# A GRU feeding a mixture of experts: gates in three stages with a bank each, one bank for transposes, and another order of the shared units' pieces

## The chip, the core and the metric

The kernel runs on one core of one Trainium2 chip. Its five engines work side by side, each through its own queue in order: TensorE (PE in the profile, with its weight loads as PEld) multiplies, VectorE (DVE) and ScalarE (ACT) do elementwise work, GpSimd (POOL) copies and issues indirect DMAs, and SyncE (SP) issues DMAs. The metric is the time of one execution on the device in microseconds; the median of three executions stands for the kernel.

## The reference

The input x has 8 sequences of 256 tokens of 512 floats. A GRU runs over the 256 steps, all 8 sequences at once; its states go through a feed-forward layer, and the result is added to x.

```python
def cell(h, x):
    gi = x @ W_ih + b_ih
    gh = h @ W_hh + b_hh
    i_r, i_z, i_n = jnp.split(gi, 3, axis=-1)
    h_r, h_z, h_n = jnp.split(gh, 3, axis=-1)
    r = jax.nn.sigmoid(i_r + h_r)
    z = jax.nn.sigmoid(i_z + h_z)
    n = jnp.tanh(i_n + r * h_n)
    h_new = (1.0 - z) * n + z * h
    return (h_new, h_new)
...
    # 8 experts of width 256, the best 2 for each token, weights renormalised
    routed = jnp.einsum('te,eth->th', combine, eo)
    shared = _silu_and_mul(x @ w_sh_gate_up) @ w_sh_down    # width 1024
    return (routed + shared).reshape(orig_shape)
```

All of it is in float32. The state of a step is needed in full before the gates of the next, so the 256 steps are a chain.

## The kernel before, in words

The 256 steps are cut into 16 blocks (k) of 16 steps: 16 steps of 8 sequences are 128 rows. The input projections (`x @ W_ih`) of a block are made while the block before runs and go out to DRAM; they come back as "seeds", four steps (a chunk) at a time, through SP's queue, a chunk ahead of their use (`load_seeds`, `turn_seeds`, lines 320 to 333). The shared part of the feed-forward layer for block k-1 is computed during block k; the routed part only after the last step, as 39 tiles of 128 rows (`tile_unit`), each with the weights of one expert. Both work on float32.

A step (`step`, lines 348 to 388) does this. TensorE multiplies the transposed state hT by the recurrent weights, in column groups of 32 that run side by side, each with a weight load of 8 columns: 16 matmuls for gates r and z together into `ps_rz` (128x256), then 16 for n into `ps_n` (128x128). In the trace each matmul is two records, so a gate group has 32. The accumulators were filled before with the input part, by copies on ScalarE (`open_gates`, lines 337 to 343), as soon as the step before had read them. Then VectorE transposes r,z (L364), ScalarE takes the sigmoid (L366), VectorE transposes n (L370), multiplies by r (L372), adds the input part (L373), ScalarE takes tanh (L375), and VectorE computes 1 - z (L379), z * h (L381), (1 - z) * n (L382) and the sum, the new state (L383). GpSimd copies it into the block's rows, `hc` (L386).

Between one step's matmuls and the next, TensorE works on pieces from a queue. The order is written out by hand at build time, not found by a scheduler: each piece has an assumed cost (0.86 for a full matmul piece, MM, and 0.12 for a transpose, TR), and in each step as many pieces are taken, whole or in halves, as spread the queue evenly over the remaining steps (lines 777 to 798). A block's queue has first the next block's projections (12 matmul pieces and the transposes of x, L245), then four shared units. A unit (`unit`, lines 570 to 605) has up to four stages: transposes of its input (only for routed tiles), four up pieces (L260, `gu_s`) with the gating on ScalarE and VectorE behind them (L566 to L568), two transposes of the activation with a copy by ScalarE (L589, L591), and two down pieces (`po`, again at L260). The fourth unit's down pieces end with an addition on VectorE (L618) and the store of the block's output by SP (L619). Some steps have routing work too: the router's matmuls (`choose`, L398), the places of tokens (L451, L453), and the transposes of the block's states (`send_rows`, L491).

`feed` (lines 709 to 719) interleaves the stages of successive units. Given a new unit, it queues the new one's first stage, then two up pieces of the unit fed before it, the transposes of the one before that, the other two up pieces, and that one's down pieces. Its calls per block are the four shared units and None, so a block's fourth unit has its transposes and down pieces as the first shared pieces of the next block, one right behind the other. Transposes take their accumulators from the pool `ps_t`, which has two buffers.

After the last step the fourth unit of block 14 and the shared units of block 15 run together with the last routing work (lines 801 to 821), and then the routed tiles.

Of the kernel before, what the change touches and what calls it, by code (L numbers as in the profile page):

```python
# [9 lines left out]
F32 = mybir.dt.float32  # L10
# [3 lines left out]
ALU = mybir.AluOpType  # L14
# [3 lines left out]
P = 128  # L18
# [7 lines left out]
def kernel(  # L26
# [42 lines left out]

    nc = tc.nc
    B, T, D = x.shape
    G3 = w_ih.shape[1]
# [20 lines left out]
    dram = ctx.enter_context(tc.tile_pool(name="dram", bufs=1, space=bass.MemoryType.DRAM))  # L95
    ps_gru = ctx.enter_context(tc.tile_pool(name="ps_gru", bufs=1, space=PSUM))
    ps_mm = ctx.enter_context(tc.tile_pool(name="ps_mm", bufs=3, space=PSUM))
    ps_t = ctx.enter_context(tc.tile_pool(name="ps_t", bufs=2, space=PSUM))
    ps_o = ctx.enter_context(tc.tile_pool(name="ps_o", bufs=1, space=PSUM))
    ctx.enter_context(tc.manual_schedule())  # L100

# [128 lines left out]

    ps_rz = ps_gru.tile([P, 2 * P], F32, name="ps_rz")
    ps_n = ps_gru.tile([P, P], F32, name="ps_n")
    for ps in (ps_rz, ps_n):
        n = ps.shape[-1]
        nc.tensor.matmul(ps, seeds[0][:, 0, 0:P], seeds[0][:, 0, 0:n], start=True, stop=True)


    xT_of = {}  # L240

    def transpose_x(k):
        ps = ps_t.tile([P, NQ, P], F32, tag="tp", name=f"xTp_{k}")
        for q in range(NQ):
            nc.tensor.transpose(ps[:, q, :], x_tiles[k][:, q * P : (q + 1) * P], ident)  # L245
        xT = two.tile([P, NQ, P], F32, tag="xrT", name=f"xT_{k}")
        nc.scalar.copy(xT, ps)  # L247
        xT_of[k] = xT
        x_tiles.pop(k)
        if k + 2 < NB:  # L250
            load_x(k + 2)

    by_groups = [True]

    def multiply(ps, lhs, rhs, start, stop):

# [77 lines left out]

    nT_of = {}

    def open_gates(n, part):

        c, t = divmod(n, SC)
        if part == 0:  # L340
            nc.scalar.copy(ps_rz, seeds[c % NS][:, t, 0 : 2 * P])  # L341
        else:
            nc.scalar.copy(ps_n, seed_hn)  # L343

    whh_v = whh.rearrange("p q (a j i) -> p q a j i", j=4, i=32)
    hc_of = {}
# [1 line left out]
    def step(n):  # L348
        k, t = divmod(n, TS)
        c, ts = divmod(n, SC)  # L350
        hT, new = states[n % NH], states[(n + 1) % NH][:, :, 0:B]
        for ps, lo, hi in ((ps_rz, 0, 2 * NQ), (ps_n, 2 * NQ, 3 * NQ)):
            for q in range(NQ):
                for j in range(4):
                    nc.tensor.matmul(  # L355
                        ps[32 * j : 32 * j + B, :].rearrange("p (a i) -> p a i", i=32),
                        hT[:, q, 0:B],
                        whh_v[:, q, lo:hi, j, :],
                        start=False,
                        stop=(q == NQ - 1),  # L360
                        skip_group_check=True,
                    )
        gT = state.tile([P, 2 * NQ, 32], F32, tag="gT", name=f"gT_{n}")
        nc.vector.transpose(gT.rearrange("p a b -> p (a b)"), ps_rz)  # L364
        rz = state.tile([P, 2 * NQ, B], F32, tag="rz", name=f"rz_{n}")
        nc.scalar.activation(rz, gT[:, :, 0:B], AF.Sigmoid)  # L366
        if n + 1 < T:
            open_gates(n + 1, 0)
        gn = state.tile([P, NQ, 32], F32, tag="gn", name=f"gn_{n}")
        nc.vector.transpose(gn.rearrange("p a b -> p (a b)"), ps_n)  # L370
        nt = state.tile([P, NQ, B], F32, tag="nt", name=f"nt_{n}")
        nc.vector.tensor_tensor(nt, gn[:, :, 0:B], rz[:, 0:NQ, :], ALU.mult)  # L372
        nc.vector.tensor_tensor(nt, nT_of[c][:, ts, :, 0:B], nt, ALU.add)  # L373
        nn = state.tile([P, NQ, B], F32, tag="nn", name=f"nn_{n}")
        nc.scalar.activation(nn, nt, AF.Tanh)  # L375
        if n + 1 < T:
            open_gates(n + 1, 1)
        omz = state.tile([P, NQ, B], F32, tag="omz", name=f"omz_{n}")
        nc.vector.tensor_scalar(omz, rz[:, NQ:, :], -1.0, 1.0, ALU.mult, ALU.add)  # L379
        zh = state.tile([P, NQ, B], F32, tag="zh", name=f"zh_{n}")  # L380
        nc.vector.tensor_tensor(zh, rz[:, NQ:, :], hT[:, :, 0:B], ALU.mult)  # L381
        nc.vector.tensor_tensor(nn, omz, nn, ALU.mult)  # L382
        nc.vector.tensor_tensor(new, nn, zh, ALU.add)  # L383
        if t == 0:
            hc_of[k] = two.tile([P, NQ, P], F32, tag="hc", name=f"hc_{k}")
        nc.gpsimd.tensor_copy(  # L386
            hc_of[k].rearrange("p q (b t) -> p q b t", t=TS)[:, :, :, t], new
        )
# [97 lines left out]
    def send_rows(k):  # L486

        hc = hc_of[k]
        ps = ps_t.tile([P, D], F32, tag="tp", name=f"hrp_{k}")
        for q in range(NQ):  # L490
            nc.tensor.transpose(ps[:, q * P : (q + 1) * P], hc[:, q, :], ident)  # L491
        hr = two.tile([P, D], F32, tag="y", name=f"hr_{k}")
        nc.scalar.copy(hr, ps)
        nc.sync.dma_start(rows[:, k * TS : (k + 1) * TS, :], hr)
# [6 lines left out]
    def lay_tiles(part_no):  # L501
# [43 lines left out]
        elif part_no == 1:  # L545
            ps = ps_mm.tile([P, NT], F32, tag="mm", name="exp")
            nc.tensor.matmul(ps, ones, laid["spread"], start=True, stop=True)
            steer = small([NT], "steer", I32)
            nc.vector.tensor_scalar(steer, ps, float(E - 1), None, ALU.min)
            laid["steer"] = steer  # L550
        else:
            ps = ps_t.tile([P, 2, P], F32, tag="tp", name="listp")
            for v in range(2):
                nc.tensor.transpose(ps[:, v, :], laid["got"][:, :, v], ident)
            row = small([NT], "row", I32)
            nc.vector.tensor_copy(row, ps[:, 0, 0:NT])
            share = small([NT], "share")
            nc.vector.tensor_copy(share, ps[:, 1, 0:NT])
            laid.update(row=row, share=share)
# [10 lines left out]
    def unit(name, box, lhs, w_up, w_down_, done, before_=None, multiply=nc.tensor.matmul):  # L570
        def up(q, cols):
            if q == 0 and cols.start == 0:
                box["ps"] = ps_mm.tile([P, 2 * IM], F32, tag="mm", name=f"gu_{name}")
            multiply(  # L574
                box["ps"][:, cols],
                lhs(q),
                w_up(q)[:, cols],
                start=(q == 0 and cols.start == 0),
                stop=(q == NQ - 1 and cols.stop == D),
            )  # L580

        def up_end():
            box["act"] = three.tile([P, IM], F32, tag="act", name=f"act_{name}")
            gated(box["ps"], box["act"])

        def turn():
            ps = ps_t.tile([P, NF, P], F32, tag="tp", name=f"actTp_{name}")
            for f in range(NF):
                nc.tensor.transpose(ps[:, f, :], box["act"][:, f * P : (f + 1) * P], ident)  # L589
            actT = two.tile([P, NF, P], F32, tag="actT", name=f"actT_{name}")  # L590
            nc.scalar.copy(actT, ps)  # L591
            box["actT"] = actT

        def down(f, cols):
            done(f, cols, box["actT"][:, f, :], w_down_(f)[:, cols])

        return (
            [(NQ * TR, before_)] if before_ else [],
            [
                matmul_piece(lambda cols, q=q: up(q, cols), up_end if q == NQ - 1 else None)  # L600
                for q in range(NQ)
            ],
            [(NF * TR, turn)],
            [matmul_piece(lambda cols, f=f: down(f, cols)) for f in range(NF)],
        )
# [47 lines left out]
    def tile_unit(i):  # L653
        box = {}

        def before_():
            ps = ps_t.tile([P, NQ, P], F32, tag="tp", name=f"xrTp_{i}")
            xr = xr_of.pop(i)
            for q in range(NQ):
                nc.tensor.transpose(ps[:, q, :], xr[:, q * P : (q + 1) * P], ident)  # L660
            xrT = two.tile([P, NQ, P], F32, tag="xrT", name=f"xrT_{i}")
            nc.scalar.copy(xrT, ps)  # L662
            box["xrT"] = xrT
            fetch_rows(i + 2)
# [44 lines left out]
    def feed(stages):  # L709
# [1 line left out]

        last, oldest = under_way["up"], under_way["turn"]
        ups = last[1] if last else []
        queue.extend(stages[0] if stages else [])
        queue.extend(ups[: NQ // 2])
        queue.extend(oldest[2] if oldest else [])
        queue.extend(ups[NQ // 2 :])
        queue.extend(oldest[3] if oldest else [])
        under_way.update(up=stages, turn=last)

    def fill():
        while queue:
# [8 lines left out]
    for c in range(NS):  # L731
        load_seeds(c)
        if c == 0:
            turn_seeds(0)
    for part_no in range(2):
        open_gates(0, part_no)
    load_shared()

    projections = deque()
# [7 lines left out]
    for k in range(NB):  # L747
# [24 lines left out]
            queue.append(projections.popleft())  # L772
        assert k == NB - 1 or len(projections) <= 13 * (NB - 2 - k), "the next block's are made"
        if k > 0:
            for u in [*(shared_unit(k - 1, c, NSH) for c in range(NSH)), None]:
                feed(u)
        over = 0.0
        for t in range(TS):
            n = k * TS + t
# [17 lines left out]
            over = -room if t < TS - 1 else 0.0  # L797
        fill()
    by_groups[0] = False

    k = NB - 1
    load_again(k)
# [7 lines left out]
        (20 * MM, lambda k: lay_tiles(2)),  # L810
        (20 * MM, lambda k: fetch_rows(0)), (20 * MM, lambda k: fetch_rows(1)),
    ]
    for u in [*(shared_unit(k, c, NSH) for c in range(NSH)), None, None]:
        feed(u)
    spent = 0.0
    while queue or routing:
        while routing and (spent >= routing[0][0] or not queue):
# [38 lines left out]
```

## Time and profile before

| | us |
|---|---|
| three executions, median (lowest to highest) | 1552.07 (1550.34 to 1553.20) |
| profiled execution | 1548.32 |
| its span, first to last instruction | 1546.5 |
| TensorE busy in the span | 1487.6 (96%) |
| VectorE, ScalarE, GpSimd busy | 688.4, 359.6, 210.5 |
| from the first gate matmul of the first step to the router's matmuls after the last | 35.7 to 1276.3 |
| first matmul of the first routed tile | 1309.5 |
| mean granted TensorE clock | 0.992 |

A row of the page's costliest groups names the line, engine and operation, what is written and read with its shape, the count, then busy time and the mean length in ns of one, and after the second bar the idle time of the engine just before, with what ended it. A row of the timeline has the start, the length, the engine, the operation, how many instructions were merged into the row, and in brackets the idle time before it with what ended it. Matmuls overlap and their ends are modelled, so the step from one start to the next is the time that TensorE spent. A row of busy times by stretch has the stretch, its length, busy time and count of TensorE, its weight loads, VectorE, ScalarE and GpSimd, then the granted clock, the share of DMA and GB/s.

### The profile page before, as it was taken

What the parts mean: (1) busy time and instruction counts of PE and PEld (TensorE: products, weight loads), DVE (VectorE), ACT (ScalarE), POOL (GpSimd) and SP (SyncE); (2) the same over time, 40 slices, a digit from 0 to 9 for tenths busy, and PEclk for the clock granted to TensorE, in tenths of its full rate; (3) what the DMA queues carried; (4) which work ended last, traced back from release to release, by engine and by line L of the source; (5) the groups of instructions that cost most, each with busy time, mean ns of one, the idle gap of its engine ahead of it and who ended that gap; (6) DMA issues with size and microseconds to landing.
All of it is one profiled execution on the core that took longest, in us unless ns stands there. A gap on an engine that the chain in (4) does not pass through costs nothing.

```text
span 1546.5 us, 53864 instructions
## 1 busy us (share of the span) xinstructions
PE 1487.6 (96%) x22969; PEld 778.0 (50%) x22969; DVE 688.4 (45%) x2747; ACT 359.6 (23%) x1351; POOL 210.5 (14%) x419
## 2 busy tenths in 40 slices
PE   4999999999999999999999999999999999999997
PEld 1455555555555555555555555555555544444443
DVE  2445454545454445454545454545454542222222
ACT  0222222222222222222222222222222221222221
POOL 2001110101000001010101010101010102444443
PEclk8999999999999999999999999999999999999998
DMA  7613130303020202010201010101010314445454
GB/s 256 201 40 108 14 87 13 100 13 101 13 60 13 60 13 59 14 52 15 57 16 50 17 41 18 48 18 48 18 53 13 84 49 135 75 89 96 84 93 62
DMA packets 59055, 92.70 MB, mean 60 GB/s; under 512 B 8960, under 2 KB 29504, under 8 KB 58816
## 3 DMA queue, kind: packets, MB, share of 16 engines
q1 hardware_dynamic: 48056, 66.89, 14.8%
q0 software_dynamic: 10624, 22.10, 7.7%
q8 instruction: 182, 2.98, 0.8%
q14 instruction: 57, 0.47, 0.1%
q10 hardware_dynamic: 136, 0.26, 0.1%
HBM read 57.85 MB, written 31.37 MB: 58 GB/s over the span
## 4 chain that ended last, share of the span: by engine, by line
PE 91%; DVE 4%; issue 2%; ACT 1%; DMA 1%; DVEq 0%; SPq 0%; POOLq 0%; POOL 0%; ACTq 0%
PE ps_rz L355 29%; PE ps_n L355 15%; PE gu_s L260 12%; PE gip L260 10%; PE gu_t L574 9%; PE po L260 6%; PE yp L679 4%; PE actTp_s L589 1%; DVE gn L370 1%; PE xrTp L660 1%; PE lgp L398 1%; ACT nn L375 1%; DMA x<-in_x_dram 1%; DVE nt L372 1%; DVE nt L373 1%
## 5 line engine op out<-in xcount | busy, mean ns | idle before, releaser
L355 PE MATMUL ps_rz<-we,hT 128*8 128x256 f32 x8192 | 491.2, 380 | 21.4 <-DVE hT L383 10.8
L355 PEld LDWEIGHTS ps_rz<-we,hT 128*8 128x8 f32 x8192 | 223.2, 89 | 298.8 <-ACT ps_n L343 56.3
L364 DVE STREAM_TRANSPOSE gT<-ps_rz 128x256 f32<-128x256 f32 x256 | 115.2, 450 | 397.2 <-PE ps_rz L355 397.1
L355 PE MATMUL ps_n<-we,hT 128*8 128x128 f32 x8192 | 271.9, 273 | 0.0
L260 PE MATMUL gu_s<-wsu,hc 128*32 128x512 f32 (+2 forms) x2376 | 257.0, 518 | 0.0
L355 PEld LDWEIGHTS ps_n<-we,hT 128*8 128x8 f32 x8192 | 225.9, 90 | 53.2 <-issue 0.5
L366 ACT ACTIVATE rz<-gT 128x64 f32<-128x64 f32 x256 | 65.6, 256 | 710.1 <-DVE gT L364 710.1
L386 POOL COPY hc<-hT 128x32 f32<-128x32 f32 x256 | 62.3, 243 | 1111.4 <-DVE hT L383 1111.4
L260 PE MATMUL gip<-we,xT 128*32 128x512 f32 (+1 forms) x1952 | 189.7, 510 | 2.1 <-ACT xT L247 2.1
L574 PE MATMUL gu_t<-we,xrT 128*128 x312 | 146.7, 593 | 0.2 <-ACT xrT L662 0.2
L260 PE MATMUL po<-wsd,actT_s 128*32 128x512 f32 (+2 forms) x1132 | 131.2, 532 | 13.3 <-ACT actT_s L591 13.3
L370 DVE STREAM_TRANSPOSE gn<-ps_n 128x128 f32<-128x128 f32 x256 | 81.1, 317 | 122.5 <-PE ps_n L355 115.2
L260 PEld LDWEIGHTS gu_s<-wsu,hc 128*32 128x32 f32 (+1 forms) x2376 | 77.2, 111 | 89.2 <-issue 79.4
L375 ACT ACTIVATE nn<-nt 128x32 f32<-128x32 f32 x256 | 58.7, 229 | 185.1 <-DVE nt L373 185.1
L341 ACT COPY ps_rz<-seeds 128x256 f32<-128x256 f32 x256 | 94.5, 369 | 22.0 <-DMA seeds<-gid_rz 21.5
L260 PEld LDWEIGHTS gip<-we,xT 128*32 128x32 f32 x1952 | 58.0, 110 | 72.2 <-issue 60.9
L567 DVE TENSOR_TENSOR act_t<-gu_t,act_t 128x256 f32<-128x256 f32 x39 | 16.6, 424 | 146.3 <-ACT act_t L566 146.3
L685 POOL DMA_INDIRECT out_dram<-y,row x39 | 61.6, 1579 | 124.7 <-DVE y L682 95.8
L679 PE MATMUL yp<-we,actT_t 128*128 x156 | 73.4, 593 | 0.5 <-ACT actT_t L591 0.5
L574 PEld LDWEIGHTS gu_t<-we,xrT 128*128 128x128 f32 x312 | 53.3, 190 | 38.7 <-issue 38.0
L260 PEld LDWEIGHTS po<-wsd,actT_s 128*32 128x32 f32 (+1 forms) x1132 | 38.0, 112 | 57.8 <-issue 33.5
L343 ACT COPY ps_n<-seed_hn 128x128 f32<-128x128 f32 x256 | 66.4, 259 | 0.0
(139 smaller groups left out, 974.1 us busy)
## 6 DMA issues: line engine op xcount, KB each, us to landing
gid_rz<-gi SPq DMA_DIRECT2D x16, 512.0 KB
seeds<-gid_rz SPq DMA_DIRECT2D x256, 32.0 KB
we<-in_L_ffn_w_gate_up_dram SPq DMA_DIRECT2D x8, 1024.0 KB
gid_n<-gi SPq DMA_DIRECT2D x16, 256.0 KB
seeds_n<-gid_n SPq DMA_DIRECT2D x256, 16.0 KB
wsu<-_L_ffn_w_sh_gate_up_dram SPq DMA_DIRECT2D x8, 512.0 KB
rows<-hr SPq DMA_DIRECT2D x16, 256.0 KB
again<-in_x_dram SPq DMA_DIRECT2D x16, 256.0 KB
```

Source lines behind the costliest of these rows:

```text
L260: nc.tensor.matmul(ps[rows_], lhs[:, rows_], rhs, start=start, stop=stop, skip_group_check=True)
L341: nc.scalar.copy(ps_rz, seeds[c % NS][:, t, 0 : 2 * P])
L343: nc.scalar.copy(ps_n, seed_hn)
L355: nc.tensor.matmul(ps[32 * j : 32 * j + B, :].rearrange("p (a i) -> p a i", i=32), hT[:, q, 0:B], whh_v[:, q, lo:hi, j, :], start=False, s ...
L364: nc.vector.transpose(gT.rearrange("p a b -> p (a b)"), ps_rz)
L366: nc.scalar.activation(rz, gT[:, :, 0:B], AF.Sigmoid)
L370: nc.vector.transpose(gn.rearrange("p a b -> p (a b)"), ps_n)
L375: nc.scalar.activation(nn, nt, AF.Tanh)
L386: nc.gpsimd.tensor_copy(hc_of[k].rearrange("p q (b t) -> p q b t", t=TS)[:, :, :, t], new)
L574: multiply(box["ps"][:, cols], lhs(q), w_up(q)[:, cols], start=(q == 0 and cols.start == 0), stop=(q == NQ - 1 and cols.stop == D),)
L679: nc.tensor.matmul(box["y"], lhs, rhs, start=(f == 0), stop=(f == NF - 1))
L685: nc.gpsimd.indirect_dma_start(out=out.rearrange("b t d -> (b t) d"), out_offset=bass.IndirectOffsetOnAxis(ap=laid["row"][:, i : i + 1], a ...
```

## The change

The gates are worked on in three stages, r, n, z, each with an accumulator of its own bank: r and z become matmuls of 128x128 like n. r's sigmoid, n and tanh, and z's sigmoid follow each behind its own transpose, and each gate's accumulator is opened for the next step on its own. The new state is n + z * (h - n), three operations on VectorE where there were four. The third bank for the gates is taken from the transposes, which have one buffer in place of two while steps run; after the last step they take the three gates' banks in turn. `feed_at_once` queues a shared unit's four up pieces at once, two ahead of the transposes of the unit before and two behind them, then that one's down pieces. So a unit's transposes wait for the next unit's up pieces, also across blocks, and the last shared unit's transposes and down pieces are queued with the first routed tile.

```diff
-    ps_t = ctx.enter_context(tc.tile_pool(name="ps_t", bufs=2, space=PSUM))
+    ps_t = ctx.enter_context(tc.tile_pool(name="ps_t", bufs=1, space=PSUM))
...
-    ps_rz = ps_gru.tile([P, 2 * P], F32, name="ps_rz")
-    ps_n = ps_gru.tile([P, P], F32, name="ps_n")
...
+    banks = {g: ps_gru.tile([P, D], F32, name=f"ps_{g}") for g in "rnz"}
...
+    def for_transposes(shape, name):
+
+        if by_groups[0]:
+            return ps_t.tile([P, *shape], F32, tag="tp", name=name)
+        spare.rotate(-1)
+        n = shape[0] * (shape[1] if len(shape) > 1 else 1)
+        bank = spare[0][:, 0:n]
+        return bank if len(shape) == 1 else bank.rearrange("p (a b) -> p a b", b=shape[1])
...
-    def open_gates(n, part):
-
+    def open_gate(n, g):
+
+        if n >= T:
+            return
         c, t = divmod(n, SC)
-        if part == 0:
-            nc.scalar.copy(ps_rz, seeds[c % NS][:, t, 0 : 2 * P])
-        else:
-            nc.scalar.copy(ps_n, seed_hn)
+        src = {"r": seeds[c % NS][:, t, 0:P], "z": seeds[c % NS][:, t, P : 2 * P], "n": seed_hn}
+        nc.scalar.copy(banks[g][:, 0:P], src[g])
...
-        for ps, lo, hi in ((ps_rz, 0, 2 * NQ), (ps_n, 2 * NQ, 3 * NQ)):
+        for g, bank in banks.items():
+            lo = "rzn".index(g) * NQ
             for q in range(NQ):
                 for j in range(4):
                     nc.tensor.matmul(
-                        ps[32 * j : 32 * j + B, :].rearrange("p (a i) -> p a i", i=32),
+                        bank[32 * j : 32 * j + B, 0:P].rearrange("p (a i) -> p a i", i=32),
                         hT[:, q, 0:B],
-                        whh_v[:, q, lo:hi, j, :],
+                        whh_v[:, q, lo : lo + NQ, j, :],
...
+        gr = turned("r")
+        r = made("r")
+        nc.scalar.activation(r, gr, AF.Sigmoid)
+        open_gate(n + 1, "r")
+        gn = turned("n")
+        nt = made("nt")
+        nc.vector.tensor_tensor(nt, gn, r, ALU.mult)
+        open_gate(n + 1, "n")
         nc.vector.tensor_tensor(nt, nT_of[c][:, ts, :, 0:B], nt, ALU.add)
-        nn = state.tile([P, NQ, B], F32, tag="nn", name=f"nn_{n}")
+        nn = made("nn")
         nc.scalar.activation(nn, nt, AF.Tanh)
...
-        nc.vector.tensor_tensor(nn, omz, nn, ALU.mult)
-        nc.vector.tensor_tensor(new, nn, zh, ALU.add)
+        gz = turned("z")
+        z = made("z")
+        nc.scalar.activation(z, gz, AF.Sigmoid)
+        open_gate(n + 1, "z")
+
+        hn = made("hn")
+        nc.vector.tensor_tensor(hn, hT[:, :, 0:B], nn, ALU.subtract)
+        nc.vector.tensor_tensor(hn, z, hn, ALU.mult)
+        nc.vector.tensor_tensor(new, nn, hn, ALU.add)
...
         last, oldest = under_way["up"], under_way["turn"]
         ups = last[1] if last else []
-        queue.extend(stages[0] if stages else [])
+        if ups:
+            queue.extend(stages[0] if stages else [])
         queue.extend(ups[: NQ // 2])
         queue.extend(oldest[2] if oldest else [])
         queue.extend(ups[NQ // 2 :])
         queue.extend(oldest[3] if oldest else [])
+        if not ups:
+            queue.extend(stages[0] if stages else [])
         under_way.update(up=stages, turn=last)
+
+    def feed_at_once(stages):
+
+
+        assert not stages[0] and under_way["up"] is None
+        under_way["up"] = stages
+        feed(None)
...
         if k > 0:
-            for u in [*(shared_unit(k - 1, c, NSH) for c in range(NSH)), None]:
-                feed(u)
+            for c in range(NSH):
+                feed_at_once(shared_unit(k - 1, c, NSH))
...
     by_groups[0] = False
+    spare.extend(banks.values())
...
-    for u in [*(shared_unit(k, c, NSH) for c in range(NSH)), None, None]:
-        feed(u)
+    for c in range(NSH):
+        feed_at_once(shared_unit(k, c, NSH))
```

The tiles of transposes in `transpose_x`, `send_rows`, `lay_tiles`, `unit` and `tile_unit` come from `for_transposes` in place of `ps_t`.

## The prediction

> **What bounds the kernel now.** I read the chain that ended last first: it says which engine to follow. Then the costliest groups, for the length of each kind of work.
>
> ```profile
> PE 91%; DVE 4%; issue 2%; ACT 1%; DMA 1%; DVEq 0%; SPq 0%; POOLq 0%; POOL 0%; ACTq 0%
> L355 PE MATMUL ps_rz<-we,hT 128*8 128x256 f32 x8192 | 491.2, 380 | 21.4 <-DVE hT L383 10.8
> L355 PE MATMUL ps_n<-we,hT 128*8 128x128 f32 x8192 | 271.9, 273 | 0.0
> ```
>
> TensorE is the chain for 91% of 1546.5 us, so only the other 9%, and whatever TensorE does at less than its pace, can be saved. Where it lies is seen only in time order, so the third view is TensorE's timeline over two recurrence steps.
>
> ```profile
> 718.01 1.06 PE L355 MATMUL ps_n<-we,hT 128*8 128x128 f32 x32
> 718.89 1.04 PE L260 MATMUL gu_s<-wsu,hc 128*32 128x512 f32 x8
> 719.75 1.04 PE L260 MATMUL po<-wsd,actT_s 128*32 128x512 f32 x8
> 720.98 1.91 PE L355 MATMUL ps_rz<-we,hT 128*8 128x256 f32 x32 [0.19 <-DVE hT L383]
> 722.71 1.06 PE L355 MATMUL ps_n<-we,hT 128*8 128x128 f32 x32
> 723.58 1.05 PE L260 MATMUL po<-wsd,actT_s 128*32 128x512 f32 x8
> ```
>
> Starts matter here, not lengths (ends are modelled and overlap). The r,z gates take 722.71 - 720.98 = 1.73 us, the n gate 723.58 - 722.71 = 0.87. Between n's last matmul and the next step come pieces of other work, each full one 0.86 (718.89 to 719.75). This step had two, 1.72 us, yet the next step began 720.98 - 718.89 = 2.09 us after n: TensorE waited about 0.37 us for hT. What made it wait is the timeline of all engines over the same stretch.
>
> ```profile
> 719.21 0.32 DVE L370 STREAM_TRANSPOSE gn<-ps_n 128x128 f32<-128x128 f32 x1 [0.50 <-PE ps_n L355]
> 719.63 0.19 DVE L372 TENSOR_TENSOR nt<-gn,rz 128x32 f32<-128x32 f32 x1
> 719.86 0.19 DVE L373 TENSOR_TENSOR nt<-nT,nt 128x32 f32<-128x32 f32 x1
> 720.08 0.23 ACT L375 ACTIVATE nn<-nt 128x32 f32<-128x32 f32 x1 [0.75 <-DVE nt L373]
> 720.35 0.19 DVE L382 TENSOR_TENSOR nn<-omz,nn 128x32 f32<-128x32 f32 x1
> 720.64 0.19 DVE L383 TENSOR_TENSOR hT<-nn,zh 128x32 f32<-128x32 f32 x1
> ```
>
> This is the tail behind the last gate matmul: transpose, multiply, add, tanh, multiply, add. I went through all 255 intervals like this one. In 91 steps the fill is two and a half pieces (2.13 us) and the tail is covered: they take 2.15. In 44 it is two pieces and they take 2.09 on average; in 6 it is one and a half and they still take 2.07. So the tail is a floor of 2.02 to 2.10 us, and it binds in about a third of the steps.
>
> Two other waits are seen in the same timelines: at the start of the shared units of a block, and after the last step.
>
> ```profile
> 762.60 0.44 PE L589 MATMUL actTp_s<-ident,act_s 128*128 128x128 f32 x2
> 763.38 0.26 ACT L343 COPY ps_n<-seed_hn 128x128 f32<-128x128 f32 x1
> 763.58 0.36 ACT L591 COPY actT_s<-actTp_s 128x256 f32<-128x256 f32 x1
> 763.99 1.50 PE L260 MATMUL po<-wsd,actT_s 128*32 128x512 f32 x16 [0.96 <-ACT actT_s L591]
> ```
>
> ```profile
> 1277.18 0.42 PE L589 MATMUL actTp_s<-ident,act_s 128*128 128x128 f32 x2
> 1280.29 3.78 PE L260 MATMUL po<-wsd,actT_s 128*128 128x512 f32 x4 [2.69 <-ACT actT_s L591]
> 1283.86 3.00 PE L260 MATMUL gu_s<-wsu,hc 128*128 128x512 f32 x4
> 1279.30:1286.10 6.80, 5.82 (x7) 2.52 (x8) 1.00 (x3) 0.55 (x3) 0.00 (x0) 0.50 0.66 252
> ```
>
> In both, a unit's transposes are followed at once by the down projection that needs their copy, and ScalarE makes that copy behind its own queue. The last line is a row of busy times by stretch: after the long idle time the granted clock is 0.50 for 6.8 us.
>
> **The change, part by part.** *Gate matmuls.* r,z of 128x256 become r and z of 128x128, 32 records each, like n: 64 in place of 32. In n, the four column groups repeat every 109.1 ns, the same for its first and last group; in r,z every 215.8. A step goes from 8 x 215.8 + 8 x 109.1 = 2.599 us to 24 x 109.1 = 2.618: 0.019 x 256 = 4.9 us more, all on the path. A rule speaks against this. The Trainium skill, "TensorE: Matmul & The Clock Gate", section "Back-to-back issue gap", gives about 81 ns for a matmul of 128 columns in a stream where each has its own weight load, against 53.3 ns of array time: a factor 1.52. Put on the 16 new groups it makes 16 x 106.7 x 1.52 = 2.59 us of what takes 1.73 now, +0.87 x 256 = +222 us, and the kernel clearly slower. The n gate is a stream of just that kind and runs at 109.1 against 106.7, its weight loads (90 ns in the groups' row) fitting in. I take the row; the rule is the upper end.
>
> *The tail.* z now comes last. The step shown above gives each term: 0.32 from the last matmul to the transpose (718.89 to 719.21), 0.32 transpose, 0.04, sigmoid of 128x32 taken at tanh's 0.23 (same shape), 0.04, multiply 0.19, 0.10, add 0.19, 0.15 to TensorE: 1.58, against 2.09 for the present tail summed in the same way. I take 1.6. What runs beside it is close behind: n is 0.87 earlier, so tanh ends 1.42 - 0.87 = 0.55 us after z's last matmul and the subtraction, which follows z's transpose on VectorE, at 0.87; the sigmoid of z ends at 0.91. r has its transpose and sigmoid done 0.91 us after its last matmul, and n's multiply wants it 0.87 + 0.74 = 1.61 after: 0.70 us of cover, the price in full beyond that.
>
> Per step VectorE does 3 x 317 + 5 x 192 = 1911 ns against 450 + 317 + 4 x 192 + 173 + 184 = 1892. ScalarE does 3 x 259 + 3 x 229 = 1464 against 369 + 259 + 256 + 229 = 1113. Both lie beside a step of 4.8 us. The wait added on VectorE (its transpose of z) holds the fill's evacuations behind it; they sat behind the whole tail before, so they come no later. The one on ScalarE (sigmoid of z, then its copy of 0.26) holds the activation copies of the fill until 1.2 us after z; they feed down projections that now come two pieces (1.7 us) later.
>
> With the floor at 1.6 each waiting step falls to its own work: two pieces, 2.09 to 1.72, 44 times: 16.1 us; one and a half, 2.07 to 1.62, 6 times: 2.7; steps with transposes or router matmuls, 35 times, counted with 0.3 us for a switch to transposes and back (2.23 for 1.92 of work where nothing waits): 4.0. Sum 22.8 us. The covered 91 gain nothing.
>
> *Units' order.* Two up pieces come before the old unit's transposes and two before its down projection. The wait of 0.96 us goes, the copy being hidden behind 1.7 us; the next in line is TensorE's own work. Such intervals average 3.23 us over 13 blocks against 2.43 of work: 10.4 us. The moved down projection takes its addition on VectorE and its store on SP's queue with it; the store then goes ahead of a different seed load, and seeds are loaded a chunk of four steps ahead, so nothing waits.
>
> *After the last step.* The idle 2.69 us is filled by the two up pieces. And the half clock: from 1280.29 to 1286.1 work for 2.9 us took 5.8. Together 5.6 us. The same page's table in "Why this matters for your kernels" warns only of idle gaps over about 3 us; the trace lost its clock with 2.69 (and 0.74 before, with nearly empty router matmuls between). By the rule only 2.7 would be saved, by the trace 5.6; I take the trace.
>
> *One bank for transposes.* No wait of a transpose for its bank is in the trace. It costs nothing where two transposes lie over 1 us apart; two fell into one fill in 1 interval of 255. Low end 0 (a wait less cannot result), high end one copy of 0.59 us in 14 blocks, 8 us; I take 0. Three banks in turn behind the loop, where TensorE waits 0.2 us in all: 0.
>
> **Sum.** 22.8 + 10.4 + 5.6 - 4.9 = 33.9 us. The profiled execution took 1548.32 (span 1546.5): 1514.4. The median is 3.75 above it: 1518.2, so 1518.
>
> **Rivals.** (1) The tail does not get that short: VectorE or ScalarE still holds work of the fill when z comes, or a dependent pair costs more. At a floor of 1.9 the 22.8 become 12.6: 1528. Left at 2.09: 1.2, hence 1540. For it: gates share VectorE with activations of 0.42 us. Against: where I looked, VectorE idles 0.9 to 2.3 us before r,z's transpose.
> (2) Slower: the stream of 24 narrow groups doesn't hold n's pace, as its weight loads (90 of 109 ns) never get ahead again. At a third of the way from row to rule, 127 ns, 16 x 0.018 x 256 = 73 us: 1591. It decides from 38.8 / 256 = 0.15 us per step, 115 ns a group. Against it: eight groups in a row show no drift.
> (3) The order of units doesn't cover the copies, as ScalarE is fuller, or the clock still falls after the last step: 10 us less at most, 1528; with the clock alone 1521.
>
> **How the numbers follow.** Main case 0.64, 1511 to 1525 with one bank's waits. Rival 1 0.18 (0.03 of it near 1540), rival 3 0.10, rival 2 0.08. 1509 to 1534 leaves out rival 2, the worst of 1 and little else. This kernel's measurement can tell 0.2% (3 us) from no change: faster 0.90, same 0.02, slower 0.08.
>
> **What would show it.** Right: gate rows for r, z and n alike, near 273 ns and 0.87 us from start to start; intervals from z to r of 1.72 where two pieces fill them, and about 1.6 where less does; no wait of po for actT_s; clock 1.00 after the last step. Wrong: group pitch above 115 ns, a new wait of TensorE for hT at 2 us, transposes waiting for ScalarE's copies, or a wait for seeds.

## The result, and the profile after

| | before | after |
|---|---|---|
| median of four executions, us (lowest to highest) | 1551.20 (1549.53 to 1553.20) | 1535.99 (1529.58 to 1538.05) |
| ratio, with its 95% interval | | 0.9897 [0.9881, 0.9912] |
| profiled execution, span, us | 1548.32, 1546.5 | 1536.72, 1534.9 |
| first gate matmul of step 0 to that of step 255 ("the loop") | 1235.8 | 1227.3 |
| from there to the first routed matmul | 38.10 | 32.19 |
| from there to the last routed matmul group | 226.17 | 226.40 |
| from there to the end | 10.82 | 12.97 |

The kernel is 1.0% faster. The forecast was 1518 (1509 to 1534), so about half of the expected gain came. By stage, in the profiled executions: the part after the last step saved 5.9 us, where 5.6 was expected. The loop saved 8.5, where 22.8 + 10.4 - 4.9 = 28.3 was expected. The end gave back 2.15.

First the page: the chain of work that ended last, and the gates' rows (the groups' columns are as before).

```profile
PE 96%; issue 1%; DMA 1%; ACT 0%; DVE 0%; SPq 0%; POOLq 0%; POOL 0%; DVEq 0%; ACTq 0%
...
L368 PE MATMUL ps_r<-we,hT 128*8 128x128 f32 x8192 | 279.1, 273 | 12.9 <-ACT ps_r L355 9.4
L368 PE MATMUL ps_n<-we,hT 128*8 128x128 f32 x8192 | 281.3, 273 | 0.8 <-issue 0.2
L368 PE MATMUL ps_z<-we,hT 128*8 128x128 f32 x8192 | 279.9, 273 | 1.4 <-issue 1.2
```

VectorE's 4% and ScalarE's 1% are gone from the chain: what TensorE waited for before, it no longer waits for. The gates run at n's pace (273 ns a record). So far the page is as forecast, and its shares don't show the loss. The timeline of TensorE over the same two-piece step as in the prediction shows the tail as planned:

```profile
718.57 1.06 PE L272 MATMUL gu_s<-wsu,hc 128*32 128x512 f32 x8
719.45 1.06 PE L368 MATMUL ps_r<-we,hT 128*8 128x128 f32 x32
720.32 1.06 PE L368 MATMUL ps_n<-we,hT 128*8 128x128 f32 x32
721.20 1.06 PE L368 MATMUL ps_z<-we,hT 128*8 128x128 f32 x32
722.07 1.04 PE L272 MATMUL gu_s<-wsu,hc 128*32 128x512 f32 x8
722.93 1.04 PE L272 MATMUL po<-wsd,actT_s 128*32 128x512 f32 x8
723.79 0.62 PE L368 MATMUL ps_r<-we,hT 128*8 128x128 f32 x16
```

Starts again: each gate 0.87 us, each piece 0.86, and r follows 1.72 after z's last, with no wait in brackets. Before, the same step took 2.09. So the loss lies elsewhere, and the waits of TensorE name it (us in total, times, longest).

```profile
PE gu_s L272 <- issue: 5.0, 4, 1.6
PE ps_r L368 <- issue: 3.1, 4, 1.5
...
PE ps_z L368 <- issue: 1.2, 6, 0.3
...
PE po L272 <- ACT actT_s L612: 0.5, 1, 0.5
```

Before, the same list had

```profile
PE po L260 <- ACT actT_s L591: 13.3, 16, 2.7
PE ps_rz L355 <- DVE hT L383: 10.8, 42, 0.7
```

So the wait for actT_s fell from 13.3 us to 0.5, and that for hT left the list. New are waits on "issue": TensorE stands still and no semaphore holds it. One of them in time order, step 6 of block 3, from the same timeline:

```profile
300.13 1.13 PE L368 MATMUL ps_r<-we,hT 128*8 128x128 f32 x30
...
303.30 1.10 PE L272 MATMUL gu_s<-wsu,hc 128*32 128x512 f32 x8
304.33 0.44 PE L610 MATMUL actTp_s<-ident,act_s 128*128 128x128 f32 x2
306.05 1.06 PE L272 MATMUL gu_s<-wsu,hc 128*32 128x512 f32 x8 [1.28 <-issue]
306.91 1.08 PE L368 MATMUL ps_r<-we,hT 128*8 128x128 f32 x32
```

This step takes 306.91 - 300.13 = 6.78 us; its work is 4.85 (shown below from another kernel). I call such a place a hole. The list of waits names only idle time between rows; where TensorE goes on with short stops, the step is longer without a bracket. So I summed, over 255 steps, the time above the pace that the step's gates and pieces have elsewhere: 24.7 us. Some 7 of it also stand in the best of the experiments (5 in block 0, of which over 2 in the very first step, at a granted clock of 0.74 from 36 to 42 us; 2 to 3 in block 15), so about 18 are left: 5.3 us in block 1 (steps 6 to 14), 2.2 in block 3, 2.6 in block 4, about 1 in block 15, and 0.3 to 0.9 in each of the others, nearly all in steps 5 and 6.

What happens there: in steps 4 to 6 the program's DMAs fall together. SP stores the block's rows (256 KB), reloads x (256 KB), loads an expert's weights (1.5 MB in blocks 1 to 4, two experts' in block 15) and in most blocks stores projections (512 and 256 KB) within a few steps of that; GpSimd writes list entries by indirect DMA from step 4 on (two in a block, eight in block 1). Busy times by stretch, with DMA share and GB/s last; the last row is the kernel before, with the same loads of the same block:

```profile
295.00:300.00 5.00, 4.96 (x128) 4.08 (x120) 2.52 (x9) 1.29 (x6) 1.14 (x2) 1.00 0.56 112
300.00:303.00 3.00, 3.00 (x101) 2.69 (x92) 0.63 (x2) 0.45 (x3) 0.98 (x1) 1.00 0.90 170
303.00:307.00 4.00, 2.54 (x25) 0.88 (x26) 1.17 (x6) 1.21 (x5) 0.24 (x1) 1.00 0.71 235
...
300.00:305.00 5.00, 4.81 (x92) 2.31 (x84) 2.33 (x9) 0.92 (x4) 1.23 (x2) 1.00 0.78 221
```

And TensorE's own instructions come by DMA. The page has a queue for them (packets, MB, share of 16 engines), here before and after:

```profile
q8 instruction: 182, 2.98, 0.8%
q8 instruction: 245, 4.01, 1.1%
```

A packet is 16 KB; 245 x 256 = 62,720 is, within 1%, the number of TensorE's matmuls and weight loads together (2 x 31,091), so a packet holds 256 instructions. The split of r,z turned 176 instructions of a step (median) into 240 (TensorE's matmuls went from 22,969 to 31,091), and in the loop the packets come every 5.0 us (median) instead of every 7.0. To see how close TensorE is to the end of its supply, take as a gauge the instructions that it has used, its control instructions included, less 256 for each earlier packet: the higher, the emptier. (Its zero is arbitrary, as the first instructions came otherwise.) When a packet starts, the gauge stands at 220 (median); when it lands, at 286. Ahead of the hole above packets start at 288.29, 293.12 and then only at 303.48: 10.4 us later, beside the bulk traffic. That one lands at 304.74 with the gauge at 449. The five latest packets of this trace, each beside a hole, all land at that same number and none above it: TensorE has used all it had and stopped. In the kernel before no packet lands above 353, so its supply never ran out. By the gauge, 449 - 220 = 229 instructions are left when a packet starts in the ordinary way; at 236 a step (mean) and 4.8 us a step that is about 4.7 us of work, an estimate.

A full DMA is not the whole of it. In block 1, where the most time above pace lies, these are two stretches with holes:

```profile
156.00:162.00 6.00, 4.74 (x111) 3.05 (x111) 1.98 (x9) 1.66 (x7) 1.23 (x2) 1.00 0.34 30
174.00:180.00 6.00, 5.55 (x161) 4.06 (x153) 2.73 (x11) 1.59 (x7) 1.22 (x2) 1.00 0.20 36
```

From 170 to 176 us nothing moves but list entries (packets of 64 and 4 bytes), and yet the next instruction packet starts at 176.07, 6.8 us after the one before, and lands with the gauge at 420. So a packet comes late beside small indirect DMAs too, with DMA nearly idle.

### The profile page after: what moved, and what is told of

It is laid out like the page before. It is cut to its first block, busy times and chain, and to the rows that moved or that the text cites. A ratio compares the mean times of both kernels' runs of the same rounds, so it can differ in the third digit from the quotient of the medians.

```text
span 1534.9 us, 70860 instructions
## 1 busy us (share of the span) xinstructions
PE 1488.7 (97%) x31091; PEld 1008.3 (66%) x31091; DVE 732.2 (48%) x2747; ACT 458.3 (30%) x1863; POOL 210.2 (14%) x419
## 4 chain that ended last, share of the span: by engine, by line
PE 96%; issue 1%; DMA 1%; ACT 0%; DVE 0%; SPq 0%; POOLq 0%; POOL 0%; DVEq 0%; ACTq 0%
PE ps_r L368 15%; PE gu_s L272 15%; PE ps_n L368 15%; PE ps_z L368 15%; PE gip L272 11%; PE gu_t L595 9%; PE po L272 7%; PE yp L700 4%; PE actTp_s L610 1%; PE lgp L419 1%; DMA x<-in_x_dram 1%; PE xTp L259 1%; PE hrp L512 1%; PE ps_z L681 0%; PE ps_n L681 0%
## 5 line engine op out<-in xcount | busy, mean ns | idle before, releaser
L368 PEld LDWEIGHTS ps_r<-we,hT 128*8 128x8 f32 x8192 | 229.1, 90 | 115.5 <-issue 53.2
L368 PE MATMUL ps_r<-we,hT 128*8 128x128 f32 x8192 | 279.1, 273 | 12.9 <-ACT ps_r L355 9.4
L368 PE MATMUL ps_n<-we,hT 128*8 128x128 f32 x8192 | 281.3, 273 | 0.8 <-issue 0.2
L368 PE MATMUL ps_z<-we,hT 128*8 128x128 f32 x8192 | 279.9, 273 | 1.4 <-issue 1.2
L272 PE MATMUL gu_s<-wsu,hc 128*32 128x512 f32 (+2 forms) x2336 | 269.2, 525 | 5.0 <-issue 5.0
L368 PEld LDWEIGHTS ps_z<-we,hT 128*8 128x8 f32 x8192 | 229.5, 90 | 3.3 <-issue 2.9
L387 ACT ACTIVATE r<-rT 128x32 f32<-128x32 f32 x256 | 58.5, 229 | 528.5 <-DVE rT L379 528.5
L379 DVE STREAM_TRANSPOSE rT<-ps_r 128x128 f32<-128x128 f32 x256 | 80.7, 315 | 262.1 <-PE ps_r L368 260.5
L379 DVE STREAM_TRANSPOSE nT<-ps_n 128x128 f32<-128x128 f32 x256 | 81.0, 316 | 138.4 <-PE ps_n L368 138.3
L379 DVE STREAM_TRANSPOSE zT<-ps_z 128x128 f32<-128x128 f32 x256 | 80.9, 316 | 12.3 <-PE ps_z L368 3.8
```

Of the source, the lines that this page charges most:

```text
L272: nc.tensor.matmul(ps[rows_], lhs[:, rows_], rhs, start=start, stop=stop, skip_group_check=True)
L368: nc.tensor.matmul(bank[32 * j : 32 * j + B, 0:P].rearrange("p (a i) -> p a i", i=32), hT[:, q, 0:B], whh_v[:, q, lo : lo + NQ, j, :], sta ...
L379: nc.vector.transpose(gT.rearrange("p a b -> p (a b)"), banks[g][:, 0:P])
L387: nc.scalar.activation(r, gr, AF.Sigmoid)
```

## The experiments

Two theories. **Supply:** the denser stream of narrow gates needs its instructions sooner than DMA brings them beside bulk loads or list entries; holes follow. **Its rivals:** the other parts cost it (the single bank of the transposes, the new order, a slower chain), or the narrow gates are themselves slower (rival 2 of the prediction). All ratios are against the kernel before, measured on the same chip in the same batch.

**1. The indirect DMAs out.** After, without the list entries of blocks 0 to 14; those rows are lost from the routed part, whose tiles still run.

```diff
-            for i in range(2 if k > 1 else E):
-                when(i + 4, 0, lambda k=k, i=i: enter(k - 1, i))
```

> The changed kernel without the list entries (the small indirect DMAs that GpSimd issues in steps 4 and 5 of each block, in steps 4 to 11 of block 1): those of blocks 0 to 14 are left out, so the routed part of the output lacks their rows; all matmuls stay. Theory A (TensorE runs out of instructions: they are fetched by DMA, the denser stream of gate matmuls uses them faster, and a fetch that falls behind another DMA comes too late; the entries are what it falls behind most often): the holes of about 0.3 to 1.9 us in steps 5 to 14 of block 1 and in steps 5 and 6 of the later blocks go, about 12 us less than the changed kernel's 1536, so 1522 to 1527. Theory B (bulk loads of 1.5 MB hold up TensorE, entries don't matter): within 2 us of 1536. Theory C (VectorE, ScalarE or the single bank for transposes make the holes): 1536.

Measured: 1523.6 (1521.0 to 1525.9), 0.9843 [0.9826, 0.9859]; loop 1211.5, which is 24.3 us less than before. The holes in blocks 1, 2 and 5 to 14 are gone or nearly so (at most 0.2 us a block), those in blocks 3 and 4 are smaller (0.7 and 1.0 us). That speaks for supply, but run 12 weakens it: the changed kernel as it stands can also run so.

**2. The split alone.** Before, with r,z's matmuls cut to 128 columns, nothing else.

```diff
-        for ps, lo, hi in ((ps_rz, 0, 2 * NQ), (ps_n, 2 * NQ, 3 * NQ)):
+        for ps, lo, hi in ((ps_rz[:, 0:P], 0, NQ), (ps_rz[:, P:], NQ, 2 * NQ), (ps_n, 2 * NQ, 3 * NQ)):
```

> The kernel before, with only r and z's matmuls of 256 columns split into two of 128 in the order r, z, n: TensorE's instruction stream becomes as dense as the changed kernel's, and nothing else changes (chain, banks, order of units). Theory A (instruction supply): 5 us from the matmuls' own pace and 8 to 18 us of holes at the same places as in the changed kernel, so 1564 to 1574. Theory C (the holes come from the engines' queues or the single bank): 5 us alone, 1556. If holes fall into steps that wait for the tail anyway, A gives its low end.

Measured: 1565.38 (1561.1 to 1569.7), 1.0114 [1.0086, 1.0142]: 16.7 us more, for which the pace of the matmuls accounts for 4.9. The rest comes without the new order, the single bank or the new chain. Step by step against the trace of the kernel before, the traced loop is 13.5 us longer: the steps that differ by no more than 0.1 us (0.02 in the median) make 5.0 of it, the 4.9 of the sum, and 14 steps with holes, most of them in blocks 0, 1 and 15, make 8.9. In two of these holes a packet lands with the gauge at 449. The loss belongs to the split.

**3. The expert's weights in sixths.** After, with each expert's 1.5 MB as six loads, one a step, in place of two in step 6.

```diff
...
-            when(6, 0, lambda k=k: load_expert(k - 1))
+            for w in range(NW):
+                when(7 + w, 0, lambda k=k, w=w: load_sixth(k - 1, w))
...
-                when(6, 0, lambda e=e: load_expert(e))
+                for w in range(NW):
+                    when(4 + w + 6 * (e - E + 2), 0, lambda e=e, w=w: load_sixth(e, w))
```

> The changed kernel with each expert's 1.5 MB load cut into six DMAs of 256 KB, one a step from step 7 (the two of block 15 from step 4). Theory B, or A with the bulk loads as the blocking DMA: the holes of 1.5 to 2 us in blocks 1, 3, 4 and 15 go, 5 to 7 us less than 1536. Theory A with the entries as the blocking DMA: 0 to 2 us less. Theory C: 1536.

Measured: 1520.0 (1516.7 to 1523.05), 0.9813 [0.9793, 0.9833], an interval clear of after's 0.9897 [0.9881, 0.9912], and about twice the gain that was expected. It leaves nothing out. But the interval of run 12, the changed kernel once more, overlaps it: two of that run's four executions took 1521. What the spreading takes away seems to be the slow executions. Same bytes, same TensorE instructions, same chain; only in what pieces and when the bytes move differs. The step of the hole above, in this kernel's timeline (its lines are five further on):

```profile
296.51 1.06 PE L373 MATMUL ps_r<-we,hT 128*8 128x128 f32 x32
297.39 1.06 PE L373 MATMUL ps_n<-we,hT 128*8 128x128 f32 x32
298.26 1.06 PE L373 MATMUL ps_z<-we,hT 128*8 128x128 f32 x32
299.13 1.04 PE L277 MATMUL gu_s<-wsu,hc 128*32 128x512 f32 x8
300.11 0.44 PE L615 MATMUL actTp_s<-ident,act_s 128*128 128x128 f32 x2
300.47 1.06 PE L277 MATMUL gu_s<-wsu,hc 128*32 128x512 f32 x8
301.36 0.84 PE L373 MATMUL ps_r<-we,hT 128*8 128x128 f32 x24
```

301.36 - 296.51 = 4.85 us in place of 6.78, with the same rows. The instruction packets around it start at 290.13, 294.56 and 299.68, never more than 6.9 us apart. Over the loop the time above pace is 8.7 us, against 24.7.

**4 and 5. Each half of the change alone.** Run 4 is before with the new `feed` and `feed_at_once`; run 5 is after with the old ones.

```diff
-        queue.extend(stages[0] if stages else [])
+        if ups:
+            queue.extend(stages[0] if stages else [])
...
-            for u in [*(shared_unit(k - 1, c, NSH) for c in range(NSH)), None]:
-                feed(u)
+            for c in range(NSH):
+                feed_at_once(shared_unit(k - 1, c, NSH))
```

> The kernel before with only the new order of the shared units (up pieces around the preceding unit's transposes); gates and banks as before. By the prediction's sum: 10.4 us from the wait of the down pieces for the copied activation in 13 blocks and 5.6 us after the last step, so 1551 - 16 = 1535, as fast as the whole change. Theory A: the same, as this stream is not denser. If part of the new order's gain was lost in the changed kernel for its own reasons: 1541 or more.

> The changed kernel with the old order of the shared units (feed for every unit and None, twice None after the last step); three gate stages and one bank for transposes stay. Theory A (the dense stream runs out of instructions where DMA traffic is heavy): the shorter tail's 22.8 us, less 4.9 for narrower matmuls, less about 20 us of holes, so near nothing: 1545 to 1551 against 1548.7 for the kernel before. Without holes it would be 1531 or less. The old order leaves waits after down pieces' transposes in which a late fetch may hide, so a little better than -2 is possible.

Measured: order alone 1536.08 (1535.7 to 1537.6), 0.9917 [0.9901, 0.9934]; gates alone 1541.32 (1538.9 to 1542.4), 0.9939 [0.9923, 0.9956], below what was expected of it. Order alone saves 5.8 us after the last step and 6.3 in the loop. The loop's 6.3 is less than the 10.4 of the sum because with the old gates a step freed of its wait for actT_s is held by the tail: the 50 steps filled with two pieces take 2.09 us there, as the 44 did before. In the changed kernel both parts are there and the two-piece steps take 1.72. Gates alone save 7.4 in the traced loop, against 22.8 - 4.9 = 17.9, with 8.9 us of waits on "issue" in its list, one of them of 3.49 us, and four packets that land at 449. So each half is worth something, and the half with the split is where the loss is.

**6. One bank for transposes.** Run 4 with `ps_t` at one buffer (here behind the loop too).

```diff
-    ps_t = ctx.enter_context(tc.tile_pool(name="ps_t", bufs=2, space=PSUM))
+    ps_t = ctx.enter_context(tc.tile_pool(name="ps_t", bufs=1, space=PSUM))
```

> The kernel before with the new order of shared units (1536.1 with two buffers for transposes) and one buffer for transposes. The prediction's value for one bank is 0, its high end 8 us: 1536 to 1537 if 0. Theory C (part of the missing gain is waits for the single bank): 1540 or more.

Measured: 1539.34 (1538.8 to 1540.1), 0.9931 [0.9914, 0.9948], between the two expectations; its interval overlaps run 4's. In the trace the loop is 0.9 us longer than run 4's (one transpose of x in step 148 waits about 0.45 us for its bank), and the stage behind the loop 2.05 (34.37 against 32.32), where the change itself has three banks. This is no place for 18 us.

**7. A control: sixths with wide gates.** Run 4 with the loads of run 3.

> The kernel before with the new order of shared units and with expert loads cut into sixths and spread over steps, as was done to the changed kernel (there 1536 to 1520). Theory A: with the sparser stream there are hardly any holes to remove (0.64 and 0.15 us seen in block 2), so 1535 to 1536. If spreading loads helps for another reason than the instruction supply, as much as in the changed kernel: about 1523.

Measured: 1535.73 (1535.4 to 1535.9), 0.9907 [0.9891, 0.9924], against 0.9917: nothing to be told apart. Spreading the loads is worth 13 us where the gates are narrow (0.9897 to 0.9813; 8, not clear of noise, against run 12's ratio) and nothing to be measured where they are wide. It doesn't help the DMAs or the chain as such; it helps the denser stream.

**8. More spreading.** Run 3, with the shared weights one a step in block 0, list entries from step 8 and the reload of x in step 13.

```diff
...
+        if k == 0:
+            for i, pair in enumerate(shared_loads):
+                when(3 + i, 0, lambda pair=pair: nc.sync.dma_start(*pair))
...
-                when(i + 4, 0, lambda k=k, i=i: enter(k - 1, i))
-            when(6, 0, lambda k=k: load_again(k - 1))
+                when(i + 8, 0, lambda k=k, i=i: enter(k - 1, i))
+            when(13, 0, lambda k=k: load_again(k - 1))
```

> The changed kernel with spread expert loads (1520.0) and also the shared weights' twelve loads one a step from step 3 of block 0, the list entries from step 8 in place of 4, and the reload of x at step 13 in place of 6. Theory A: the holes left (2.5 us in steps 2 and 3 of block 0, 2.7 in block 1, about 1 in block 15) shrink: 1514 to 1518. If they stay at 1520, the holes left aren't caused by these loads.

This missed: 1523.07 (1522.1 to 1523.25), 0.9827 [0.981, 0.9843]. The holes didn't go: those in block 1 stayed, and block 15, where the traffic now stands later, has more (4.1 us, 1.4 in run 3). In its step 11:

```profile
1231.07 0.40 PE L373 MATMUL ps_n<-we,hT 128*8 128x128 f32 x7
1233.58 1.64 PE L373 MATMUL ps_n<-we,hT 128*8 128x128 f32 x25 [2.10 <-issue]
1234.82 2.11 PE L373 MATMUL ps_z<-we,hT 128*8 128x128 f32 x32
```

A gate's matmuls break off after seven. An instruction packet starts at 1230.93, 7.3 us after the one before it; the gauge stands at 449 again when it lands. z's matmuls then run from 1234.82 to 1236.52, 1.70 us for 0.87 of work. Where traffic falls seems to matter, not only how it is cut.

**9. Entries one a block.** Run 3, with block 0's eight list entries in step 14 of blocks 1 to 8. Entries that come late overwrite those of later blocks, so a part of the routed rows is lost.

```diff
-            for i in range(2 if k > 1 else E):
+            for i in range(2 if k > 1 else 0):
...
+            if k <= E:
+                when(14, 0, lambda k=k: enter(0, k - 1))
```

> The changed kernel with expert loads in sixths over the steps (1520.0) and block 0's eight list entries spread one a block over blocks 1 to 8 (at step 14) instead of eight in a row in block 1. Theory A: the 2.7 us of holes in block 1 go, 1516 to 1519. If the holes only move elsewhere, as they did when more loads were moved (1523): 1519 to 1523.

Measured: 1517.01 (1515.0 to 1520.0), 0.9788 [0.9771, 0.9805]; block 1 has no time above pace (run 3: 2.6 us), and the loop is 1209.3, 26.4 us under before.

**10. The split alone, with sixths.** Run 2 with the loads of run 3.

> The kernel before with r and z's matmuls split in two (1565.4, 16.7 over the kernel before, of which 4.9 is the matmuls' pace), and the expert loads in sixths over the steps. Theory A: a good part of the 12 us of holes goes, 1554 to 1560. If the cost of the split is in the matmuls or weight loads themselves and not in late instructions: 1565 as before.

Measured: 1560.39 (1558.7 to 1566.1), 1.0065 [1.0049, 1.0082], just clear of run 2's 1.0114 [1.0086, 1.0142]. By the medians the split costs less in the kernel before, too, when the loads are spread, but not only its 4.9 us. The profiled execution is its slowest (1566.08) and no shorter than run 2's: its hole in step 7 of block 15, where expert loads stood, is 0.6 us in place of 3.7, but one of 5.2 us stands in step 8 of block 1, beside the list entries, which this run left in place.

**11. Sixths and no entries.** Runs 1 and 3 together; the rows of run 1 are lost.

> The changed kernel with expert loads in sixths and without the list entries of blocks 0 to 14 (left out, so the routed part of the output lacks their rows; all matmuls stay). Theory A: only the first steps' holes (2.4 us, loads of the shared weights) and about 1 us in block 15 stay; 1515 to 1518, which is the recorded sum of 1518 with nothing left of the instruction supply. If other causes hold the loop: 1520 or more, as with each alone.

Measured: 1519.75 (1519.1 to 1520.2), 0.9807 [0.979, 0.9823]; loop 1210.1. No better than run 3 by the interval, and short of the 1515 to 1518 expected of supply alone: two remedies for one ill. What remains lies in blocks 0 and 15.

**12. The changed kernel again,** beside runs 9 to 11.

> The changed kernel once more, beside the three others: 1531 to 1538 if its kernel before is at 1549; its holes again in blocks 1, 3, 4 and 15 and at steps 5 and 6 of the others. In its first measurement the loop lost about 20 us to them; 15 to 22 is expected.

Measured: 1526.77, 0.9867 [0.9826, 0.9908], from four executions at 1520.9, 1532.54, 1533.72 and 1521.0: faster than expected, with fewer holes. The profiled one is that of 1520.9. Its loop takes 1213.7, its time above pace is 10.9 us, and step 6 of block 3, 6.78 us above, takes 4.84 here; its packets start at 289.94 and 295.79. Above those 7 us that even the best run has, the same program thus lost some 4 us to holes in one traced execution and some 18 in the other. On this chip the kernel before spread by 2.0 us in seven executions, this one by 12.8 in four. That is what a supply at its edge looks like; a slower matmul, a bank or an order would be expected to cost the same each time.

## Why the prediction was right in its mechanism and wrong in its time

- **The step that failed** is "Gate matmuls": "0.019 x 256 = 4.9 us more, all on the path". The pace was right: 0.873 us a gate in every step without a hole, 24 groups in a row as 8 were. What was left out is that 64 more instructions a step have to be brought to TensorE. In the profiled execution the loop came out 19.8 us above the sum (28.3 - 8.5), in run 12's 6.2 (28.3 - 22.1). Measured alone (run 2), the split costs 16.7 us: the 4.9 of pace, and holes. The page of before had the row that should have been asked (q8, 182 packets); I counted durations, and the new instructions only as time on TensorE. How far the total misses is partly chance: four executions gave 1535.99, just outside the stated range, and the ratio of the four in run 12 makes about 1531 of the same kernel, inside it.
- **Rival 2** said that the stream of 24 narrow groups doesn't hold its pace. It doesn't, but not as told: the weight loads fit, the pitch of 109 ns stood, and the price comes in bursts of 0.3 to 3.5 us beside bulk loads and list entries. Averaged, 19.8 / 256 = 0.08 us a step, half of the 0.15 from which that rival would have made it slower. (Its 73 us counts 16 groups, its limit of 115 ns all 24; with 24 the 73 would be 110.) In run 2, where nothing pays for it, the split is slower. The rule of about 81 ns, which was rejected, is not what came.
- **The tail** was right. Two-piece steps take 1.72 (49 steps, median), and the floor shows in the five steps of one and a half pieces without routing: 1.56, against 2.07 before; I had taken 1.6. Rival 1 (a floor of 1.9 or more) is out.
- **The order of units** was right: the wait for actT_s went from 13.3 us to 0.5. What that is worth in the changed kernel was not measured apart; alone it brought 6.3 of its 10.4 us (run 4). Rival 3 is out, by this and by the next point.
- **After the last step**, 5.9 us for 5.6: by the trace's reading and not by the rule of 3 us. The up pieces stand where the idle time was, and the granted clock is 1.00 in the whole stretch from 1268 to 1286:

```profile
1268.07 1.06 PE L419 MATMUL lgp<-wg,hc 128*128 128x8 f32 x8 [0.59 <-POOL hc L407]
1268.99 1.96 PE L272 MATMUL gu_s<-wsu,hc 128*128 128x512 f32 x4
1270.79 0.38 PE L610 MATMUL ps_n<-ident,act_s 128*128 128x128 f32 x2
1271.00 1.88 PE L272 MATMUL gu_s<-wsu,hc 128*128 128x512 f32 x4
```

- **One bank**, taken at 0 with a high end of 8: about 1 in run 6.
- **The sum** with the supply mended: the loops of runs 1, 3, 11 and 9 are 24.3, 24.3, 25.7 and 26.4 us under before. The other terms made 28.3, so the rest of the sum holds within 2 to 4 us, and blocks 0 and 15 still have time above pace for that.
- **The end** gave back 2.15 us that I had not counted. The last tile's y is ready 11.6 us before the end, 9.4 in the kernel before; its scatter to the output starts 5.1 us after y, 3.1 before, as on GpSimd's queue it comes behind the scatters ahead of it. This last stage took 12.43 in run 3, 10.98 in run 12 and 10.79 in run 8, so it is not the change as such. Why it varies stays open.

Open too: what decides in one execution of the unchanged program whether a packet comes just in time or just too late. The packets' starts show that it does; nothing in the trace says why, nor how list entries of 64 bytes can hold a packet up. And the step from "packet late beside traffic" to "late because of it" rests on runs 3, 9 and 10, which changed only the traffic, with intervals that lie close together; no run delayed the packets alone.

## What to carry to other kernels

A smaller matmul costs its instructions too: before cutting one in two, count TensorE's instructions per microsecond and look how far apart the instruction packets lie, and what else DMA carries there, small indirect DMAs included. If TensorE stands still on "issue", look at the loads of that moment; spreading 1.5 MB over six steps was worth 8 to 13 us here (the 8 not clear of noise), while moving more of the traffic to later steps gained nothing. And where a program sits at such an edge, one trace is not enough: the same kernel showed 8.5 us of gain in the loop in one execution and 22.1 in another.

## What the runs showed of the hardware

TensorE's own instructions come through DMA, and they can run out: in all ten traces with narrow gates the latest packet lands with the gauge at exactly 449, in the four with wide gates at 353 to 443. After a hole the granted clock can fall. Run 5 stands still for most of 4 us in block 15 (the columns as above, the clock third from the end):

```profile
1225.00:1229.00 4.00, 0.62 (x15) 0.48 (x18) 0.00 (x0) 0.00 (x0) 0.00 (x0) 0.76 1.03 382
1229.00:1233.00 4.00, 4.00 (x70) 2.99 (x66) 1.41 (x6) 1.11 (x6) 0.00 (x0) 0.50 0.49 187
```

DMA is full (a share of 1.03, 382 GB/s), TensorE has 0.62 us of work, and the clock is 0.50 for the 4 us behind it. In run 8 a hole of 2.1 us was followed by 0.60 in the 3 us from 1233; in the hole shown first, with 1.28 us idle, the clock stayed at 1.00. So a late packet can be paid for twice, as the idle time after the last step was in the kernel before.
